# One scan sequence over eight images, and a bound on where TensorE's other products may stand between its state sums

## The chip, the cores and the metric

The kernel runs on one core of one Trainium2 chip. The time is the device time of one execution in microseconds, and the profile is that of one further execution on the same core. All arithmetic is float32.

## What is computed

The reference is a chain of four layers on a batch of eight images of 384 channels and 32x32 pixels. Layer 0 is a state-space block (Mamba) run in both directions over the 1024 pixels, with a gated local branch. Layer 1 is a pointwise and depthwise convolution, linear attention and an MLP. Layers 2 and 3 are large depthwise convolutions (folded into one 13x13 kernel each), a pointwise product and a GELU. Cut to what the kernel's stages show:

```python
# layer 0, per image and direction; d = 384 channels, n = 16 states
xz = einsum('blc,ec->ble', x, in_proj_w);  u, z = split(xz, 2)
u = silu(causal_conv4(u) + b)
dt, Bm, Cm = split(einsum('blc,ec->ble', u, x_proj_w), [24, 40])
delta = softplus(dt @ dt_proj_w.T + dt_proj_b)
h = exp(delta * A) * h + delta * u * Bm      # a scan over 1024 pixels
y = (einsum('bdn,bn->bd', h, Cm) + u * D) * silu(z)
x = x + res_scale * (xn * sigmoid(dwconv3(xn) + dw_b) + scale_mod * (y @ out_proj_w.T))
# layer 1
x = x + c2(dwconv3(c1(x)));  x = x + proj(linear_attention(qkv(x)))
x = x + gelu(layernorm(x) @ w1 + b1) @ w2 + b2
# layers 2 and 3
x = sum of seven depthwise convolutions with batch norm
x = pointwise(x) + x;  out = gelu(dwconv13(x) + scaled x)
```

## The kernel before

All work of layers 0 and 1 is written out by one Python function, `_layers01`, and a compile-time scheduler decides the order of the instructions of each engine: it follows priorities in program order and its own estimate of when inputs are ready, and it puts in the semaphores. [...] The lists are fixed when the program is built.

**The scan of one image.** `scan(b)` walks over 12 units: direction d, half h of the pixels (512 columns), chunk c of 128 channels. A unit has four rounds, so an image has 48 rounds and the batch 384. A round handles four of the sixteen states. Its work is, for each of two halves i:

- ScalarE computes `da`, the exponentials of delta times A, in two instructions of 128x512 (L776), from `dlt`. The tag `da` has 4 buffers, two rounds' worth.
- VectorE multiplies `vr` by the broadcast `bct` into `du`, which lies in PSUM (L781), and runs two scans of 128x512 into `hs` (L793). In the first half of the pixels it copies the end state to `carry` (L798).
- GpSimd multiplies `hs` by the other part of `bct` (L802). The tag `hs` has 8 buffers, four rounds' worth.
- TensorE adds the four states of each channel with four packed products of 128x32 (L736) into `acc`; this is `sums`, and it runs two rounds late, from the list `late`. At the first round of a unit `acc` also takes `y0` (L741). After the unit's fourth round `acc` is copied out (direction 0, `yt`, L746) or multiplied by the gate and stored as `g` (direction 1, L749 and L750).

The scan's inputs are loaded by SP's DMA queue: `load` brings `dlt` and `vr` of the next unit (tag `rep`), `load_bc` the rows `bct`. At the end of an image the two remaining `sums` are written out, and the next image's `scan` starts with its own loads.

**The other work.** While image b is scanned, two generators are advanced: `front(b + 1)`, which is layer 0 ahead of the scan (norm `ms`, products `in`, the local branch `lc` and `lg` at L611 to L620, the causal convolution `c`, `xd`, `dt`, the softplus at L671 to L678, and the stores of delta at L685), and `layer1(b - 1)`, which is the end of layer 0 (`op`, from `g`) and all of layer 1 (`h`, `dw`, `c2`, the attention's `kv_kp`, `kv_vt`, `kvs`, `q`, `den`, `rzb`, `pj`, then `mu`, `var`, and the MLP's `mf` and `mo`). Each yields a cost after a piece of work. `fold` and `kernels` prepare weights during the first images. The driver advances them by a common ratio after each round:

```python
while work and done < need * (i + 1) / (rounds - 1):
    w = min(work, key=lambda w: w[2] / w[1])
    cost = next(w[0], None)
```

`tick` runs small pieces that were put off by `defer`. What a round writes out of this work is thus set by the driver, but where the scheduler then puts it on TensorE's list is not bound to the round.

**After the scans.** `layer1` of image 7 runs alone, and then layers 2 and 3 as convolutions from Toeplitz blocks (`cv_a`, `pw`, `cv_b`, L316 and L347).

[...]

Of the kernel before, what the change touches and what calls it, by code (L numbers as in the profile page):

```python
# [1 line left out]

# [6 lines left out]
FP = mybir.dt.float32  # L9
AF = mybir.ActivationFunctionType  # L10
ALU = mybir.AluOpType
# [3 lines left out]
P = 128  # L15
C = 384
NC = C // P
# [3 lines left out]
HALF = 512  # L21
# [353 lines left out]
def _layers01(tc, nc, B, xv, x2_d, dram, ident, mean_w, eps5, eps6, one, half, minus1, vec, bns, bnt,  # L375
# [12 lines left out]
    with ExitStack() as ctx:  # L388
        wp = ctx.enter_context(tc.tile_pool(name="w0", bufs=1))
        sp = ctx.enter_context(tc.tile_pool(name="s0", bufs=2))  # L390
# [28 lines left out]
        def const(ap, shape, tag):  # L419
            t = wp.tile(shape, FP, tag=tag, name=tag)  # L420
            nc.scalar.dma_start(t, ap)
            return t
# [9 lines left out]
            nc.gpsimd.memset(spread[32 * j : 32 * j + 1, j, :], 1.0)  # L432
        t1 = const(taps1, [P, 2 * NG, 32], "t1")
        selt = const(sel, [P, 32], "selt")
        neg_a = const(alog, [P, NG, NR], "neg_a")
        nc.scalar.activation(neg_a, neg_a, AF.Exp)
        nc.vector.tensor_scalar_mul(neg_a, neg_a, -1.0)
# [55 lines left out]
        def tick(everything=False):  # L493
            for e in list(late):
                e[0] -= 1
                if e[0] < 0 or everything:
                    late.remove(e)
                    e[1]()

        def dense(ps, w, m, rhs):  # L500
            for k in range(NC):
# [14 lines left out]
        def rows(t):  # L516
            return t.rearrange("p (h w) -> p h w", w=W)
# [54 lines left out]
        def front(b):  # L572

            xn = []
# [34 lines left out]
            for h in range(2):  # L609
                for c in range(NC):  # L610
                    xr = t2(f"xr_{b}_{h}_{c}")  # L611
                    nc.sync.dma_start(xr, xv[b][:, c, bass.ts(h, HALF)])
                    ps = conv3(xn_d, b % 2, h, c, t3, f"lc_{b}_{h}_{c}")
                    lc = t2(f"lg_{b}_{c}_{h}")
                    nc.scalar.activation(lc, ps, AF.Sigmoid, bias=vec("dw_b0", c))

                    def local(h=h, c=c, lc=lc, xr=xr):
                        nc.vector.tensor_mul(rows(lc), rows(lc), xn[h][c])
                        nc.vector.scalar_tensor_tensor(xr, lc, rs, xr, ALU.mult, ALU.add)
                        nc.gpsimd.dma_start(x1v[b][:, c, bass.ts(h, HALF)], xr)  # L620

                    defer(1, local)
                    yield 3
# [68 lines left out]
                    defer(1, deltas)  # L692
                    yield 3

        def scan(b):

            units = [
                (d, h, c)
                for d in range(2) for h in ((0, 1) if d == 0 else (1, 0)) for c in range(NC)
            ]  # L700
            late = []
# [2 lines left out]
                return t.rearrange("p (j n) -> p j n", n=HALF)  # L704

            def load_bc(k, r):
                d, h, _ = units[k]
                t = sp.tile([P, 2, HALF], FP, tag="bct", name=f"bct_{b}_{d}_{h}_{r}", bufs=4)
                for o in range(2):
                    src = bass.AP(  # L710
                        bc_d.tensor, bc_d[b, d, o * NST + 4 * r, h * HALF].offset,
                        [[0, 32], [L, 4], [1, HALF]],
                    )
                    nc.sync.dma_start(t[:, o, :], src)
                return t

            def load(k, i):

                d, h, c = units[k]
# [12 lines left out]
            def sums(k, r, hs, acc, y0, zt):  # L732
                d, h, c = units[k]
                cols = bass.ts(h, HALF)
                for j in range(4):
                    nc.tensor.matmul(  # L736
                        acc[32 * j : 32 * j + 32, :], selt, hs[j // 2][:, bass.ts(j % 2, HALF)],
                        start=(r == 0), stop=(r == NR - 1), skip_group_check=True,
                    )
                if r == 0:  # L740
                    nc.tensor.matmul(acc, ident, y0, start=False, stop=False, skip_group_check=True)  # L741
# [13 lines left out]
            for k, (d, h, c) in enumerate(units):  # L755
                cols = bass.ts(h, HALF)
                second = k % (2 * NC) >= NC
                for r in range(NR):
# [11 lines left out]
                    end = HALF - 1 if d == 0 else 0  # L770
                    for i in range(2):
                        dlt, vt = now[i]
                        da = sp.tile([P, 2 * HALF], FP, tag="da", name=f"da_{b}_{k}_{r}_{i}", bufs=N_DA)
                        for j in range(2):
                            g = 4 * c + 2 * i + j
                            nc.scalar.activation(  # L776
                                da[:, bass.ts(j, HALF)], dlt[:, bass.ts(j, HALF)], AF.Exp,
                                scale=neg_a[:, g, r : r + 1],
                            )
                        du = accp.tile([P, 2 * HALF], FP, tag="du", name=f"du_{b}_{k}_{r}_{i}")  # L780
                        nc.vector.tensor_mul(  # L781
                            pairs(du), pairs(vt),
                            bct[r][:, 0:1, :].to_broadcast([P, 2, HALF]),
# [5 lines left out]
                        t = sp.tile([P, 2 * HALF], FP, tag="hs", name=f"hs_{b}_{k}_{r}_{i}", bufs=N_HS)  # L789
# [86 lines left out]

        def layer1(b):

            xx = []
            w = wtile(outproj_t, f"wo_{b}")  # L880
            for h in range(2):
                xh, gh = a6(f"xx_{b}_{h}"), a6(f"g_{b}_{h}")
                nc.sync.dma_start(xh, x1v[b][:, :, bass.ts(h, HALF)])
                nc.sync.dma_start(gh, gv[b][:, :, bass.ts(h, HALF)])
                xx.append(xh)
                for m in range(NC):
                    ps = long_psum(f"op_{b}_{m}_{h}")
                    dense(ps, w, m, gh)
                    o = xh[:, m, :]
                    nc.vector.scalar_tensor_tensor(o, ps, rsm, o, ALU.mult, ALU.add)  # L890
                    yield 3
            w = wtile(c1_d, f"c1_{b}")
            for h in range(2):
# [195 lines left out]
            tick()  # L1089
        tick(everything=True)  # L1090
        rounds = 4 * NC * NR
        for b in range(B):
            work = []
            if b + 1 < B:
                work.append([front(b + 1), 90, 0])
            if b > 0:
                work.append([layer1(b - 1), 325, 0])
            if b == 0:
                work.append([fold(), 30, 0])
            if b == 1:  # L1100
                work.append([some(prepare, 7), 1, 0])
            elif b > 1:
                work.append([some(prepare, 6), 12, 0])
            need = sum(n for _, n, _ in work)
            done = 0
            for i, _ in enumerate(scan(b)):
                tick()

                while work and done < need * (i + 1) / (rounds - 1):
                    w = min(work, key=lambda w: w[2] / w[1])  # L1110
                    cost = next(w[0], None)
                    if cost is None:
                        work.remove(w)
                        continue
                    w[2] += cost
                    done += cost
            for w in work:
                for _ in w[0]:
                    tick()
            tick(everything=True)  # L1120
        for _ in prepare:
            pass
        for _ in layer1(B - 1):
# [90 lines left out]
```

## Time and profile before

| | us |
|---|---|
| three runs | 5799.74, 5803.92, 5806.63 |
| median | 5803.92 |
| the profiled execution | 5806.88 |
| its span, first to last instruction | 5805.1 |
| first scan of image 0 | 215.6 |
| first scan of image 1 | 735.4 |
| first scan of image 7 | 4164.3 |
| last scan of image 7 | 4648.0 |
| granted clock of TensorE, mean | 0.896 of full |
| table loads of ScalarE | 776 of 1.283 |

Engines are PE (TensorE products), PEld (its weight loads), DVE (VectorE), ACT (ScalarE), POOL (GpSimd) and SP (the queue of most loads). A number such as L736 is a line of the kernel before. In the list of 40 slices each digit is the busy share of a fortieth of the span (145 us) in tenths. A wait is written as who waited, an arrow, and the work that ended the wait. A `sums` product is recorded as two instructions, as is every product here. The start of a round is the start of its first scan (L793) in the timeline of VectorE.

### The profile page before, as it was taken

Reading aid. Unit: us, or ns where it says so; the run is one execution under the profiler, and the core shown is the slowest. Engines: PE = TensorE matmul, PEld = TensorE weight load, DVE = VectorE, ACT = ScalarE, POOL = GpSimd, SP = SyncE. Lnnn points to the kernel's source line nnn. Section 1 sums busy time; section 2 is a strip of 40 time slices with the busy share of each in tenths; the row PEclk is TensorE's granted clock in tenths of the full one; section 3 lists DMA queues with packets and bytes.
Section 4 is the critical chain, followed back from the end, with each engine's and each line's share of the span. In section 5 each row is a group of like instructions: output and inputs, shape, how many; then the busy total and the mean of one; then the engine's idle time right before and its main releaser. Section 6 shows DMA issues by size and latency. Waiting matters only on the chain. (4 is left out here: it accounts for less than half of the span.)

```text
span 5805.1 us, 57844 instructions
## 1 busy us (share of the span) xinstructions
PE 4813.5 (83%) x19550; PEld 2091.8 (36%) x19550; DVE 3677.1 (63%) x3775; ACT 3064.5 (53%) x4116; POOL 2892.9 (50%) x1603
## 2 busy tenths in 40 slices
PE   4576579977988799879888997899779869899999
PEld 1121124322332243223322332233223324498498
DVE  0399997968687768776878786878678811011211
ACT  1656546874667557846784687468635613000211
POOL 3277676557554656565656564656466700110133
PEclk7687689988999899989999998899889989999999
DMA  9555476677567756764666467646643541366677
GB/s 299 185 176 178 145 247 194 230 188 216 187 197 202 216 173 193 168 204 134 191 205 189 141 175 186 190 140 176 179 145 120 135 96 45 95 165 158 196 166 150
DMA packets 528255, 1012.16 MB, mean 174 GB/s; under 512 B 60616, under 2 KB 196248, under 8 KB 527960
## 3 DMA queue, kind: packets, MB, share of 16 engines
q1 hardware_dynamic: 387952, 665.99, 38.5%
q0 software_dynamic: 71136, 248.53, 16.6%
q10 hardware_dynamic: 68872, 93.95, 5.1%
q8 instruction: 155, 2.54, 0.2%
q14 instruction: 140, 1.15, 0.1%
HBM read 763.86 MB, written 288.36 MB: 181 GB/s over the span
## 5 line engine op out<-in xcount | busy, mean ns | idle before, releaser
L802 POOL TENSOR_TENSOR hs<-hs,bct 128x1024 f32<-128x1024 f32 x768 | 2378.7, 3098 | 1180.4 <-DVE hs L793 665.8
L776 ACT ACTIVATE da<-dlt,neg_a 128x512 f32<-128x512 f32 x1536 | 1031.7, 714 | 848.8 <-DVE hs L793 756.8
L793 DVE TENSOR_TENSOR_SCAN hs<-da,carry,du 128x512 f32<-128x512 f32 x768 | 947.1, 1268 | 445.8 <-PE acc L736 211.0
L781 DVE TENSOR_TENSOR du<-vr,bct 128x1024 f32<-128x1024 f32 x768 | 1048.3, 1365 | 51.7 <-issue 21.7
L793 DVE TENSOR_TENSOR_SCAN hs<-da,du 128x512 f32<-128x512 f32 x768 | 901.2, 1208 | 153.9 <-ACT da L776 74.0
L736 PE MATMUL acc<-hs,selt 128*32 128x512 f32 x3072 | 736.5, 674 | 293.0 <-POOL hs L802 241.7
L1064 PE MATMUL mo<-hm,w 128*128 128x512 f32 x1152 | 562.5, 628 | 84.4 <-ACT hm L1062 60.8
L502 PE MATMUL mf<-ln,w 128*128 128x512 f32 x1152 | 545.7, 614 | 42.8 <-ACT dl L672 40.4
L736 PEld LDWEIGHTS acc<-hs,selt 128*32 128x32 f32 x3072 | 122.3, 115 | 722.2 <-POOL hs L802 391.6
L1064 PEld LDWEIGHTS mo<-hm,w 128*128 128x128 f32 x1152 | 214.9, 197 | 427.8 <-issue 255.1
L776 ACT ACT_TABLE_LOAD x265 | 340.0, 1283 | 39.2 <-DVE hs L793 26.7
L502 PEld LDWEIGHTS mf<-ln,w 128*128 128x128 f32 x1152 | 215.2, 194 | 358.9 <-issue 285.1
L316 PE MATMUL cv_b<-xt_b,toep 128*64 128x256 f32 x2688 | 304.5, 388 | 14.1 <-DVE xt_b L298 14.1
L316 PE MATMUL cv_a<-xt_a,toep 128*64 128x256 f32 x2688 | 304.6, 388 | 9.2 <-DVE xt_a L298 9.2
L502 PE MATMUL in<-xn,win 128*128 128x512 f32 x576 | 289.1, 633 | 26.0 <-ACT phi_k L874 24.2
L511 PE MATMUL dw<-dw_i,t3b 96*32 96x512 f32 x1152 | 238.0, 707 | 86.4 <-DMA dw_i<-h_d 86.3
L316 PEld LDWEIGHTS cv_b<-xt_b,toep 128*64 128x64 f32 x2688 | 282.5, 199 | 36.6 <-issue 16.2
L316 PEld LDWEIGHTS cv_a<-xt_a,toep 128*64 128x64 f32 x2688 | 282.4, 199 | 31.1 <-issue 10.4
L511 PE MATMUL lc<-lc_i,t 96*32 96x512 f32 x1152 | 218.1, 679 | 57.2 <-issue 28.8
L511 PE MATMUL c<-ut,t 128*32 128x512 f32 x768 | 195.2, 676 | 45.6 <-DMA ut<-u_d 32.1
L502 PE MATMUL op<-g,wo 128*128 128x512 f32 x288 | 143.1, 647 | 86.7 <-DMA g<-g_d 58.7
L1062 ACT ACTIVATE hm<-mf,biasf 128x512 f32<-128x512 f32 x192 | 130.7, 687 | 145.2 <-PE mf L502 143.5
(189 smaller groups left out, 5618.3 us busy)
## 6 DMA issues: line engine op xcount, KB each, us to landing
dlt<-dl_d SPq DMA_DIRECT2D x384, 256.0 KB, 4.5
vr<-v_d SPq DMA_DIRECT2D x384, 256.0 KB, 4.7
bct<-bc_d SPq DMA_DIRECT2D x256, 256.0 KB, 4.1
ut<-u_d SPq DMA_DIRECT2D x192, 257.5 KB, 5.0
lc_i<-xn_d SPq DMA_DIRECT2D x192, 228.8 KB, 4.9
dw_i<-h_d SPq DMA_DIRECT2D x192, 228.8 KB, 4.1
tp_d<-g_d POOLq DMA_DIRECT2D x64, 672.0 KB, 7.2
w<-w_d SPq DMA_DIRECT2D x64, 576.0 KB, 5.8
```

The lines of the kernel that those rows point to most:

```text
L316: nc.tensor.matmul(ps[2 * H * e : 2 * H * (e + 1), 0:BW], tp[:, 2 * (g % (GB // 2)) + e, :, :, t].rearrange("p c j -> p (c j)"), rhs, star ...
L502: nc.tensor.matmul(ps, w[:, k, m * P : (m + 1) * P], rhs[k] if isinstance(rhs, list) else rhs[:, k, :], start=(k == 0), stop=(k == NC - 1),)
L511: nc.tensor.matmul(ps[32 * j : 32 * j + 32, :], lhs(j, i), rhs(j, i), start=(i == 0), stop=(i == taps - 1), skip_group_check=True,)
L736: nc.tensor.matmul(acc[32 * j : 32 * j + 32, :], selt, hs[j // 2][:, bass.ts(j % 2, HALF)], start=(r == 0), stop=(r == NR - 1), skip_group ...
L776: nc.scalar.activation(da[:, bass.ts(j, HALF)], dlt[:, bass.ts(j, HALF)], AF.Exp, scale=neg_a[:, g, r : r + 1],)
L781: nc.vector.tensor_mul(pairs(du), pairs(vt), bct[r][:, 0:1, :].to_broadcast([P, 2, HALF]),)
L793: nc.vector.tensor_tensor_scan(t[:, s][:, way], da[:, s][:, way], du[:, s][:, way], k_c if second else 0.0, ALU.mult, ALU.add,)
L802: nc.gpsimd.tensor_mul(pairs(t), pairs(t), bct[r][:, 1:2, :].to_broadcast([P, 2, HALF]))
L1062: nc.scalar.activation(hm, ps, AF.Gelu, bias=biasf[:, NC * i + f, :])
L1064: nc.tensor.matmul(acc[m], wb[:, f, m * P : (m + 1) * P], hm, start=(i == 0 and f == 0), stop=(i == FF // C - 1 and f == NC - 1),)
```

## The change

There are five edits.

1. `scan` becomes one generator over all 8x12 units. The loads of the next image's first unit are written out in the last rounds of the image before, as between any two units, and the `sums` of the last two rounds of an image are written out in the first rounds of the next.
2. In TensorE's order, products of the other work that are written out after round i are placed behind the `sums` that stand second to last in the list `summed` at that time (`LAG` = 1), which are those of round i-3. The four products of each `sums` are placed behind the last TensorE instruction of the other work written out two rounds before (`BEHIND` = 2), that is, in the same round as the scan that they add up. Both are edges for the scheduler on one engine's list; no semaphore is added for them.
3. Each generator of the driver has its own pace between a first and a last round: `front` from 0 to 43, `layer1` from 3 to 47. At round 43 everything deferred is written out.
4. `layer1` takes half 1 before half 0 in its first two products, `op` and `h`.
5. The sigmoid of the local branch is written as a tanh: sigmoid(v) = (1 + tanh(v/2))/2. The product with `xn` takes the added one, and the residual takes half the scale. Four multiplies of one column at the start make the halved constants.

The core of the diff:

```diff
+LAG = 1
+BEHIND = 2
...
+        def order(ins, before):
+            tc.add_manual_dep(
+                ins, before.name,
+                mybir.DependencyInfo(mybir.DependencyClass.NoSync, mybir.DependencyReason.DATA),
+            )
...
-                    nc.scalar.activation(lc, ps, AF.Sigmoid, bias=vec("dw_b0", c))
+                    nc.scalar.activation(lc, ps, AF.Tanh, bias=dwh[:, c, :], scale=0.5)
...
-                        nc.vector.tensor_mul(rows(lc), rows(lc), xn[h][c])
-                        nc.vector.scalar_tensor_tensor(xr, lc, rs, xr, ALU.mult, ALU.add)
+                        nc.vector.scalar_tensor_tensor(
+                            rows(lc), rows(lc), one, xn[h][c], ALU.add, ALU.mult
+                        )
+                        nc.vector.scalar_tensor_tensor(xr, lc, rsh, xr, ALU.mult, ALU.add)
...
-        def scan(b):
+        def scan():
             units = [
-                (d, h, c)
+                (b, d, h, c) for b in range(B)
                 for d in range(2) for h in ((0, 1) if d == 0 else (1, 0)) for c in range(NC)
             ]
...
+                after = between[-BEHIND] if len(between) >= BEHIND else []
                 for j in range(4):
-                    nc.tensor.matmul(
+                    ins = nc.tensor.matmul(
                         acc[32 * j : 32 * j + 32, :], selt, hs[j // 2][:, bass.ts(j % 2, HALF)],
                         start=(r == 0), stop=(r == NR - 1), skip_group_check=True,
                     )
+                    for o in after:
+                        order(ins.ins, o)
...
+                summed.append(ins.ins)
...
-            for h in range(2):
+            for h in (1, 0):
                 xh, gh = a6(f"xx_{b}_{h}"), a6(f"g_{b}_{h}")
...
+        last = rounds - NR + 1
+        summed = []
+        between = []
+        scans = scan()
         for b in range(B):
             work = []
             if b + 1 < B:
-                work.append([front(b + 1), 90, 0])
+                work.append([front(b + 1), 90, 0, last - 2, 0])
             if b > 0:
-                work.append([layer1(b - 1), 325, 0])
+                work.append([layer1(b - 1), 325, 3, rounds - 1, 0])
...
+            for i in range(rounds):
+                next(scans)
                 tick()
+                ends = []
+                with tc.issue_after(summed[-1 - LAG]) if len(summed) > LAG else nullcontext():
+                    for w in list(work):
+                        gen, need, lo, hi, done = w
+                        at = len(traced())
+                        while done < need * (i + 1 - lo) / (hi - lo) or i >= hi:
+                            cost = next(gen, None)
...
+                        mine = [t for t in traced()[at:] if t.engine == mybir.EngineType.PE]
+                        if mine:
+                            ends.append(mine[-1])
+                between.append(ends)
+                if i == last - 2:
+                    tick(everything=True)
```

More of the change, by code (lines that the diff above doesn't have):

```diff
@@ L1 @@
-from contextlib import ExitStack
+from contextlib import ExitStack, nullcontext
 import concourse.bass as bass
@@ L434, in _layers01 @@
         selt = const(sel, [P, 32], "selt")
+        dwh = wp.tile([P, NC, 1], FP, tag="dwh", name="dwh")
+        for c in range(NC):
+            nc.vector.tensor_scalar_mul(dwh[:, c, :], vec("dw_b0", c), 0.5)
+        rsh = wp.tile([P, 1], FP, tag="rsh", name="rsh")
+        nc.vector.tensor_scalar_mul(rsh, rs, 0.5)
         neg_a = const(alog, [P, NG, NR], "neg_a")
@@ L498, in tick, with traced @@
                     e[1]()
+        def traced():
+            return nc.cur_bb.bb.instructions
+        def order(ins, before):
[3 more added lines that the diff above has]
+            )
         def dense(ps, w, m, rhs):
@@ L706, in load_bc @@
             def load_bc(k, r):
-                d, h, _ = units[k]
+                b, d, h, _ = units[k]
                 t = sp.tile([P, 2, HALF], FP, tag="bct", name=f"bct_{b}_{d}_{h}_{r}", bufs=4)
@@ L717, in load @@
             def load(k, i):
-                d, h, c = units[k]
+                b, d, h, c = units[k]
                 ts = []
@@ L732, in sums @@
             def sums(k, r, hs, acc, y0, zt):
-                d, h, c = units[k]
+                b, d, h, c = units[k]
                 cols = bass.ts(h, HALF)
+                after = between[-BEHIND] if len(between) >= BEHIND else []
                 for j in range(4):
-                    nc.tensor.matmul(
+                    ins = nc.tensor.matmul(
                         acc[32 * j : 32 * j + 32, :], selt, hs[j // 2][:, bass.ts(j % 2, HALF)],
@@ L739, in sums @@
                     )
+                    for o in after:
+                        order(ins.ins, o)
                 if r == 0:
-                    nc.tensor.matmul(acc, ident, y0, start=False, stop=False, skip_group_check=True)
+                    ins = nc.tensor.matmul(acc, ident, y0, start=False, stop=False, skip_group_check=True)
+                summed.append(ins.ins)
                 if r < NR - 1:
@@ L754, in scan @@
             acc = y0 = zt = nxt = None
-            for k, (d, h, c) in enumerate(units):
+            for k, (b, d, h, c) in enumerate(units):
                 cols = bass.ts(h, HALF)
@@ L772, in scan @@
                         dlt, vt = now[i]
-                        da = sp.tile([P, 2 * HALF], FP, tag="da", name=f"da_{b}_{k}_{r}_{i}", bufs=N_DA)
+                        da = sp.tile([P, 2 * HALF], FP, tag="da", name=f"da_{k}_{r}_{i}", bufs=N_DA)
                         for j in range(2):
@@ L779, in scan @@
                             )
-                        du = accp.tile([P, 2 * HALF], FP, tag="du", name=f"du_{b}_{k}_{r}_{i}")
+                        du = accp.tile([P, 2 * HALF], FP, tag="du", name=f"du_{k}_{r}_{i}")
                         nc.vector.tensor_mul(
@@ L788, in scan @@
                             bct[NR - 1] = load_bc(k, NR - 1)
[L789 removed]
+                        t = sp.tile([P, 2 * HALF], FP, tag="hs", name=f"hs_{k}_{r}_{i}", bufs=N_HS)
                         for j in range(2):
@@ L877, in layer1 @@
         def layer1(b):
-            xx = []
+            xx = [None, None]
             w = wtile(outproj_t, f"wo_{b}")
-            for h in range(2):
+            for h in (1, 0):
                 xh, gh = a6(f"xx_{b}_{h}"), a6(f"g_{b}_{h}")
@@ L884, in layer1 @@
                 nc.sync.dma_start(gh, gv[b][:, :, bass.ts(h, HALF)])
-                xx.append(xh)
+                xx[h] = xh
                 for m in range(NC):
@@ L892, in layer1 @@
             w = wtile(c1_d, f"c1_{b}")
-            for h in range(2):
+            for h in (1, 0):
                 hh, mid = image6(f"hh_{b}_{h}")
@@ L1094, in _layers01 @@
             if b + 1 < B:
-                work.append([front(b + 1), 90, 0])
+                work.append([front(b + 1), 90, 0, last - 2, 0])
             if b > 0:
-                work.append([layer1(b - 1), 325, 0])
+                work.append([layer1(b - 1), 325, 3, rounds - 1, 0])
             if b == 0:
-                work.append([fold(), 30, 0])
+                work.append([fold(), 30, 0, rounds - 1, 0])
             if b == 1:
-                work.append([some(prepare, 7), 1, 0])
+                work.append([some(prepare, 7), 1, 0, last, 0])
             elif b > 1:
[L1103 to L1106, printed above, removed]
+                work.append([some(prepare, 6), 12, 0, rounds - 1, 0])
+            for i in range(rounds):
+                next(scans)
                 tick()
[L1109 to L1120, printed above, removed]
+                ends = []
[5 more added lines that the diff above has]
+                            cost = next(gen, None)
+                            if cost is None:
+                                work.remove(w)
+                                break
+                            done += cost
+                            w[4] = done
+                        mine = [t for t in traced()[at:] if t.engine == mybir.EngineType.PE]
[4 more added lines that the diff above has]
+                    tick(everything=True)
+        next(scans, None)
+        tick(everything=True)
         for _ in prepare:
```

## The prediction

> **What bounds the kernel now.** I read, in this order: the busy shares and the 40 slices, the windows by image and by stretch, the waits of VectorE, the timeline of VectorE where it stands longest, and the order of the built programs.
>
> ```profile
> span 5805.1 us, 57844 instructions
> PE 4813.5 (83%) x19550; PEld 2091.8 (36%) x19550; DVE 3677.1 (63%) x3775; ACT 3064.5 (53%) x4116; POOL 2892.9 (50%) x1603
> ...
> PE   4576579977988799879888997899779869899999
> ...
> DVE  0399997968687768776878786878678811011211
> ACT  1656546874667557846784687468635613000211
> ```
>
> From slice 3 to slice 32 no engine is full: TensorE, VectorE and ScalarE share the load and wait for each other. This is the scan stage, 8 images of 48 rounds, 215.6 to 4648.0 us in the timeline. A round of the scan (two `du`, four scans) costs VectorE 2x1.365 + 4x1.24 = 7.7 us by the rows of L781 and L793, and the shortest rounds last 7.6 us; 48 of them would be 365 us, while images 1 to 6 take 3428.9/6 = 571.5 us each. The next view is VectorE's waits in these six images (735.4 to 4164.3 us): us in all, times, longest.
>
> ```profile
> DVE hs L793 <- ACT da L776: 236.6, 79, 16.4
> DVE hs L793 <- PE acc L736: 218.6, 48, 19.1
> DVE dl L683 <- ACT sp L678: 59.8, 22, 11.0
> DVE xx L890 <- PE op L502: 41.5, 7, 17.7
> ```
>
> Half of what the scan waits for is TensorE's state sums (they free the `hs` buffers), half is ScalarE's exponentials. The windows of image 5, cut after rounds 11, 20 and 35 (columns: length, then busy of PE, PEld, DVE, ACT, POOL, then clock, DMA):
>
> ```profile
> 3023.90:3132.50 108.60, 85.21 (x332) 29.86 (x333) 102.61 (x119) 61.22 (x92) 81.35 (x41) 0.86 0.66 210
> 3132.50:3260.00 127.50, 112.03 (x399) 48.45 (x393) 78.04 (x62) 60.68 (x93) 60.11 (x27) 0.93 0.41 124
> 3260.00:3417.00 157.00, 146.20 (x562) 51.72 (x564) 139.81 (x153) 116.92 (x144) 95.49 (x38) 0.92 0.63 194
> 3417.00:3589.40 172.40, 150.55 (x435) 49.32 (x432) 117.95 (x103) 140.69 (x169) 95.25 (x52) 0.94 0.68 175
> ```
>
> The first stretch is VectorE's, the second TensorE's, the last ScalarE's. The second holds one round of 42 us, which VectorE's timeline shows:
>
> ```profile
> 3203.99 2.45 DVE L793 TENSOR_TENSOR_SCAN hs<-da,carry,du 128x512 f32<-128x512 f32 x2 [18.90 <-PE acc L736]
> 3206.47 1.23 DVE L781 TENSOR_TENSOR du<-vr,bct 128x1024 f32<-128x1024 f32 x1
> 3220.88 2.45 DVE L793 TENSOR_TENSOR_SCAN hs<-da,carry,du 128x512 f32<-128x512 f32 x2 [13.17 <-PE acc L736]
> ```
>
> In the order of the program before, 116 products of other images stand between the sums of rounds 12 and 13; the scan, four rounds of `hs` buffers ahead, runs into them at round 16. That is the loss the change can reach.
>
> [...] the trace has 1283 ns on every load and the next activation about 0.02 us behind it, so I price 1.283. [...]
>
> **The change part by part.** Loads of each engine are counted from the built order (what stands between one round's scan work and the next on that engine) times durations of this trace: a 128x512 product 2x0.429 us at full clock and divided by 0.93, four packed sums 0.9, a table load 1.283, other work by its row.
>
> *Table sets.* Sigmoid becomes tanh: 776 loads become 676 in the built programs, 128 us of ScalarE, some 13 us per image of 397. The activation stays (0.687 us at L615). The product at L618 (mean 1490 ns) becomes a fused one like L619 (824 ns): 48 of them, between 0 and 32 us of VectorE, inside the loads below; I take 0. Four multiplies of one column (like L158, 0.16 us) lie under the first image's front.
>
> *One sequence.* Loads for the next image's first unit, eight of 256 KB, and its `bct` move from after an image's end to its rounds 45 to 47 on SP's queue; they land in 4.1 to 4.7 us, and the `rep` and `bct` buffers come free at the scan's pace as inside an image. [...] The stores of the front that they read (POOL's queue, behind a 3.1 us multiply each) are flushed at round 43. I cost the move at 0. Rounds 0 and 1 lasted 16 and 12 to 29 us, partly by the 41.5 us on `op`; `layer1` now begins at round 3, with the half whose `g` was stored three units earlier, so that wait goes (it is inside the stretches below).
>
> *The binding.* Products lie at most about three rounds ahead of the sums; the largest block between sums is 49 small ones. By stretches of a steady image, load before (and what it lasted) and after, in us, the largest engine:
> - before: rounds 0-11 DVE 116 (108.6); 12-20 PE 129 (127.5); 21-35 DVE 152 (157); 36-47 ACT 147 (172.4).
> - after: rounds 0-8 DVE 86 (PE 83); 9-20 PE 109 (DVE 100); 21-30 DVE 112 (PE 94); 31-43 ACT 188 (DVE 126, PE 119); 44-47 DVE 41.
>
> The first three stretches before lasted 0.99 of their largest load (393 of 397), so rounds 0 to 30 after give 0.99x307 = 304. Two things are added. First, what the binding costs: sums of round r now stand behind the products traced with round r. In eleven rounds (nine of 9-20, and 27, 28) the built semaphores make sums r wait, through ScalarE's order, for a scan of round r+3, while scan r+4 needs sums r: no slack. The long chain is two exponentials 1.4, a square 0.6, two kv products 3.9, kvs and sums 1.5, six hand-overs of an estimated 0.2 (a weight load is 0.19): 8.6, and 2.5 of scan, 11.1 us a round, some 3.2 over what VectorE needs; the short chain is 7.1 and free. All short costs 0, nine long 29; half, **14 us**. Second, ScalarE's stretch: 188 us at 1.17 (as 172.4/147) is 220, at full density 188; TensorE is lighter there than before (119 in 13 rounds, where it was busy 151 of 172), so I take the middle, **203**. Sum: 304 + 14 + 203 + 41 = **562 us**, against 571.5: -9.5, six times, **-57**.
>
> *Image 7* has `layer1` alone: its rounds 0-1 lasted 43 us and 12-15 72 us, with loads of 20 and 44 in the new order; less 16 us of the chain, **-35** (-15 to -45). Image 0 (450 and 452 us of VectorE), `layer1` of the last image and the convolutions stay: 0.
>
> Sum -92. The profiled run took 5806.88 us (span 5805.1), the median of three is 5803.92, 3 less: 5803.9 - 92 = **5712 us**. Ends per image: 304+0+188+41 = 533 (-231 and -45: 5528) and 304+29+220+41 = 594 (+135 and -15: 5924).
>
> **The rivals.**
> 1. *The order was the only loss*: chain hidden, ScalarE dense; 533 per image, 5528 to about 5560. For it: TensorE is level in the new order. Against: ScalarE's own density in the last stretch is 141 of 172.
> 2. *Slower: the binding turns TensorE's waits into the scan's.* In rounds 8 to 20 sums stand behind products that wait for ScalarE or for `dw` images (TensorE waited 122 us in all for these, 15 per image, formerly with other products to run). Chain 29 and dw 15 on top of 304+203+41: 592, +20.5 six times, less 20 for image 7: +103, about **5905**. It decides from some 29 us per image. For it: eleven rounds without slack. Against: rounds without slack also stand in the MLP of image 7 before and last 7.6 to 10 us.
> 3. *ScalarE takes over*: 1.17 holds, 579 per image, +45-35: 5814, no change.
> 4. *The binding does nothing*: excluded by the built order (116 to 49).
>
> **How the numbers follow.** Forecast 0.38, rival 1 0.20, rival 3 0.10, rival 2 0.32. Below 0.2% (12 us) no measurement of this kernel tells a change. Faster 0.58, within 0.09, slower 0.33. The likeliest case alone spans 5640 to 5780; the 8-in-10 range, 5570 to 5880, cuts the outer parts of rivals 1 and 2.
>
> **What would show it.** Right: VectorE's wait for `acc` in images 1 to 6 falls from 218.6 to about 100 and no round is over 25 us; table loads 676; rounds 31-43 last 190 to 220 us with ScalarE the busiest; the wait for `da` does not fall. Wrong: rounds 9-20 above 140 us (rival 2), or rounds 31-43 below 185.

## The result, and the profile after

The changed kernel is slower. It takes 6067.73 us (median of four runs, 6058.21 to 6077.94), the kernel before on the same chip 5805.16: a ratio of 1.0454, 95% interval 1.0434 to 1.0475. The forecast was 5712 with a range up to 5880, so the result lies past the range and past the slower rival (5905). The profiled execution took 6062.94 us.

The head of the page after, and three of its rows of 40 slices:

```profile
span 6061.2 us, 57648 instructions
PE 4853.6 (80%) x19550; PEld 2093.5 (35%) x19550; DVE 3649.8 (60%) x3779; ACT 2921.7 (48%) x4016; POOL 2939.3 (48%) x1603
...
PE   5565568876878788878897887788769879899899
...
DVE  0488976858675867686778686768678821011211
ACT  1644525674457645754595568456834623100211
```

The engines do nearly the same work as before: TensorE is busy 40 us more (its granted clock was 0.880 on average, before 0.896), GpSimd 46 us more, VectorE 27 us less, ScalarE 143 us less (the hundred table loads that are gone, at 1.283 us each 128 us). So most of the 256 us of span are waiting, not work. By parts, from first scan to first scan:

| part | before | after |
|---|---|---|
| before the first scan | 215.6 | 219.8 |
| image 0 | 519.8 | 533.6 |
| images 1 to 6 | 3428.9 | 3657.7 (609.6 each, before 571.5) |
| image 7 | 483.7 | 489.0 |
| after its last scan | 1157.1 | 1161.1 |

Nine tenths of the loss are in the six steady images. The next table gives the mean length of stretches of an image there, in us, cut where the two kernels differ.

| rounds | 0-9 | 10-13 | 14-22 | 23-30 | 31-43 | 44-47 | sum |
|---|---|---|---|---|---|---|---|
| before | 109 | 36 | 112 | 98 | 159 | 58 | 572 |
| after | 94 | 71 | 93 | 122 | 196 | 33 | 609 |

Three stretches became shorter, 59 us together: the start of an image, the stretch with the 42 us round, and the end. Three became longer, 97 us together. What is awaited there stands in TensorE's waits of the changed kernel in images 1 to 6 (753.4 to 4411.1 us; us in all, times, longest):

```profile
PE dw L528 <- DMA dw_i<-h_d: 138.4, 27, 24.9
PE c L528 <- DMA ut<-u_d: 115.6, 15, 21.6
PE mo L1090 <- ACT hm L1088: 93.8, 51, 11.1
PE var_b L581 <- ACT var_r L578: 66.7, 12, 7.7
PE lc L528 <- DMA t<-in_taps: 51.2, 6, 10.4
```

Before, the same two rows for `dw` and `ut` read as follows, and `lc` had none for its weights `t`:

```profile
PE dw L511 <- DMA dw_i<-h_d: 63.3, 29, 5.5
PE c L511 <- DMA ut<-u_d: 23.3, 13, 3.5
```

The three waits for a DMA grew by about 218 us together, and the six images by 229. That the two are close proves nothing, since the rows of `mo` and `var_b` grew as well (from 40.7 and 25.8); what the waits cost is for the experiments to say. The six images in VectorE's waits of the changed kernel:

```profile
DVE hs L819 <- PE acc L759: 349.8, 69, 17.5
DVE hs L819 <- ACT da L802: 263.1, 80, 26.6
DVE lg L635 <- ACT lg L632: 115.1, 12, 20.0
DVE xx L946 <- ACT c L943: 100.4, 18, 10.5
```

The wait for the sums has risen from 218.6 to 349.8 instead of falling to 100. The last two rows are new near the top: VectorE itself stands behind the gate of the local branch (`lg`, fed by `lc`) and the residual after `c2` (fed by `dw`), with scans queued behind them. Rounds of over 25 us, of which the forecast expected none, are 13 in these six images, where there were 9; most are round 12, 23, 38 or 39.

**Rounds 11 and 12**, 21.2 and 23.5 us in image 5. The timeline of all engines there, of which I show the DMA issues, and then TensorE's own (start, length, operation, and in brackets the idle time ahead and what ended it):

```profile
3296.94 0.38 ACTq L547 DMA_DIRECT2D h_d<-hh  x1
...
3301.63 3.78 SPq L558 DMA_DIRECT2D dw_i<-h_d  x6
```

```profile
3307.02 6.22 PE L528 MATMUL dw<-dw_i,t3b 96*32 96x512 f32 x27 [15.16 <-DMA dw_i<-h_d]
...
3320.48 1.92 PE L528 MATMUL dw<-dw_i,t3b 96*32 96x512 f32 x2 [4.41 <-DMA dw_i<-h_d]
```

`h` goes to DRAM at 3296.9, comes back as shifted images from 3301.6, and the first product starts at 3307.0: 10 us of round trip. TensorE has stood for 15 us by then, since this product is next on its list. Only six images are on their way at once (the tag `im` has 6 buffers, and a product takes four), so the next products wait too (4.41 us). VectorE in the same rounds:

```profile
3320.63 1.23 DVE L807 TENSOR_TENSOR du<-vr,bct 128x1024 f32<-128x1024 f32 x1
3335.57 2.45 DVE L819 TENSOR_TENSOR_SCAN hs<-da,carry,du 128x512 f32<-128x512 f32 x2 [13.71 <-PE acc L759]
```

The scan waits 13.71 us for sums that stand behind `dw`.

**Round 23**, 28.0 us in image 5 and 28 to 36 in the six, is the wait for the tap weights `t` of `lc`. TensorE stands for them, and VectorE then waits for the gate that the `lc` products feed; the next scan, at 3488.3 us, is behind this gate in its order. First TensorE, then VectorE's row of `lg` between 3455 and 3492 us:

```profile
3471.28 5.68 PE L528 MATMUL lc<-lc_i,t 96*32 96x512 f32 x28 [8.87 <-DMA t<-in_taps]
```

```profile
DVE lg L635 <- ACT lg L632: 15.8, 2, 9.1
```

**Round 38**, 34.5 us. The x2 stores leave on POOL's queue and the loads of `ut` on SP's, at the same time:

```profile
3669.66 2.33 POOL L1102 DMA_DIRECT2D x_d<-xx  x2
...
3673.06 3.56 SPq L656 DMA_DIRECT2D ut<-u_d  x4
...
3698.02 3.81 PE L528 MATMUL c<-ut,t 128*32 128x512 f32 x4 [20.42 <-DMA ut<-u_d]
...
3704.67 1.28 DVE L819 TENSOR_TENSOR_SCAN hs<-da,carry,du 128x512 f32<-128x512 f32 x1 [25.91 <-ACT da L802]
```

A `ut` load has a median of 4.9 us over the whole program. These four took 24.9 to 26.2 us to land, TensorE stands for 20.42, and the scan 25.91. The scan does not wait for these products; ScalarE's timeline shows how it comes to them:

```profile
3701.86 0.69 ACT L664 ACTIVATE uc<-c,pk 128x512 f32<-128x512 f32 x1 [22.99 <-PE c L528]
3702.57 1.28 ACT L802 ACT_TABLE_LOAD   x1
3703.86 0.72 ACT L802 ACTIVATE da<-dlt,neg_a 128x512 f32<-128x512 f32 x1
```

The exponentials stand behind the activation of `c` in ScalarE's order, and that waits 22.99 us; their own row shows no wait. One late load thus stops three engines in turn, for 20.42, 22.99 and 25.91 us.

The windows of image 5, cut after rounds 11, 20 and 35 (columns as in the prediction), answer to those shown of before:

```profile
3218.20:3335.60 117.40, 87.24 (x342) 31.23 (x342) 97.30 (x113) 49.79 (x77) 81.32 (x35) 0.88 0.63 199
3335.60:3444.00 108.40, 101.03 (x372) 41.06 (x370) 73.36 (x60) 60.93 (x89) 59.72 (x26) 1.00 0.41 129
3444.00:3636.00 192.00, 164.45 (x634) 57.39 (x632) 148.16 (x160) 115.47 (x151) 100.39 (x42) 0.91 0.56 179
3636.00:3806.10 170.10, 131.96 (x380) 45.54 (x378) 114.41 (x105) 135.38 (x167) 94.39 (x55) 0.89 0.61 168
```

Only the second, the attention's rounds, was improved by more than a few us (127.5 to 108.4), and TensorE is again busy for most of it. In the third no engine is full.

### The profile page after: what moved, and what is told of

Read it like the earlier page. It is cut to its first block, busy times and chain, and to the rows that moved or that the text cites. A ratio compares the mean times of both kernels' runs of the same rounds, so it can differ in the third digit from the quotient of the medians.

```text
span 6061.2 us, 57648 instructions
## 1 busy us (share of the span) xinstructions
PE 4853.6 (80%) x19550; PEld 2093.5 (35%) x19550; DVE 3649.8 (60%) x3779; ACT 2921.7 (48%) x4016; POOL 2939.3 (48%) x1603
## 5 line engine op out<-in xcount | busy, mean ns | idle before, releaser
L828 POOL TENSOR_TENSOR hs<-hs,bct 128x1024 f32<-128x1024 f32 x768 | 2427.5, 3161 | 1563.3 <-DVE hs L819 760.7
L807 DVE TENSOR_TENSOR du<-vr,bct 128x1024 f32<-128x1024 f32 x768 | 1005.3, 1309 | 26.7 <-DMA vr<-v_d 14.5
L759 PE MATMUL acc<-hs,selt 128*32 128x512 f32 x3072 | 642.6, 646 | 215.5 <-POOL hs L828 196.4
L1090 PE MATMUL mo<-hm,w 128*128 128x512 f32 x1152 | 579.1, 643 | 118.5 <-ACT hm L1088 118.5
L519 PE MATMUL mf<-ln,w 128*128 128x512 f32 x1152 | 558.9, 623 | 23.5 <-ACT dl L691 23.5
L528 PE MATMUL lc<-lc_i,t 96*32 96x512 f32 x1152 | 233.6, 746 | 128.3 <-DMA t<-in_taps 51.2
L759 PEld LDWEIGHTS acc<-hs,selt 128*32 128x32 f32 x3072 | 96.0, 111 | 609.8 <-POOL hs L828 337.6
L635 DVE SCALAR_TENSOR_TENSOR lg<-lg,one,xn 128x512 f32<-128x512 f32 x48 | 72.9, 1519 | 258.4 <-ACT lg L632 243.0
```

The lines of the kernel that those rows point to most:

```text
L519: nc.tensor.matmul(ps, w[:, k, m * P : (m + 1) * P], rhs[k] if isinstance(rhs, list) else rhs[:, k, :], start=(k == 0), stop=(k == NC - 1),)
L528: nc.tensor.matmul(ps[32 * j : 32 * j + 32, :], lhs(j, i), rhs(j, i), start=(i == 0), stop=(i == taps - 1), skip_group_check=True,)
L635: nc.vector.scalar_tensor_tensor(rows(lc), rows(lc), one, xn[h][c], ALU.add, ALU.mult)
L759: ins = nc.tensor.matmul(acc[32 * j : 32 * j + 32, :], selt, hs[j // 2][:, bass.ts(j % 2, HALF)], start=(r == 0), stop=(r == NR - 1), skip ...
L807: nc.vector.tensor_mul(pairs(du), pairs(vt), bct[r][:, 0:1, :].to_broadcast([P, 2, HALF]),)
L828: nc.gpsimd.tensor_mul(pairs(t), pairs(t), bct[r][:, 1:2, :].to_broadcast([P, 2, HALF]))
```

## The experiments

All ratios are to the kernel before, run on the same chip at the same time, with 95% intervals. The kernel before took 5763 to 5810 us on the chips used, so where two changed kernels are set against each other, it is their ratios that are compared.

### Which edit costs: the two edges and the tanh

`e1_unbound` keeps all of the change but the edges (edit 2):

```diff
-                after = between[-BEHIND] if len(between) >= BEHIND else []
+                after = []
...
-                with tc.issue_after(summed[-1 - LAG]) if len(summed) > LAG else nullcontext():
+                with nullcontext():
```

> The changed kernel with both edges on TensorE's order taken out: one sequence, own paces, half 1 first and tanh stay. Theory A (the binding makes TensorE's waits for DMA-fed images the scan's waits): most of the 262 us go, 5780 to 5860 us, and TensorE's wait for dw images and ut images (254 us over images 1 to 6 in the changed kernel) falls to under 130. Theory B (writing the next image's loads and the paces into one sequence costs by itself): 6000 to 6070. Theory C (ScalarE's order in rounds 31 to 43 decides): within 1% of the changed kernel, since ScalarE's work is the same.

Measured 1.0305 [1.0281, 1.0328], 5940.45 us, which fits none of the three theories: the loss is neither all in the edges nor untouched by them. TensorE's waits in images 1 to 6 show what the edges do:

```profile
PE c L528 <- DMA ut<-u_d: 118.5, 23, 21.6
PE dw L528 <- DMA dw_i<-h_d: 44.3, 18, 6.8
PE lc L528 <- DMA t<-in_taps: 23.2, 4, 7.5
```

With the edges `dw` waits 138.4 and `lc` 51.2 us. The wait for `ut` is as long without them (115.6 with), so it has another cause.

`e2_lag_only` has only the first of these two edits and so keeps only the bound on how far ahead the other products may stand; `e3_behind_only` has only the second and keeps the bound on how far behind; `e4_behind4` sets `BEHIND = 4`.

> The changed kernel with only the edge that puts the sums behind the other products (BEHIND) taken out; other products still may not run ahead of the sums by more than three rounds. Theory A: the sums need not wait for a product that waits for DMA, but a late product can still stand ahead of them by the scheduler's choice: 5800 to 5900. Theory B: 6000 to 6070. Theory C: within 1% of the changed kernel.

> The changed kernel with only the other edge (LAG) taken out; sums still stand behind the products written out in the round of their scan. Theory A: as slow as the changed kernel or slower, 6030 to 6150, since this edge is the one that ties the sums to a late product. Theory B: 6000 to 6070. Theory C: within 1%.

> The changed kernel with BEHIND = 4: sums of round r stand behind the products of round r-2 instead of r. Theory A: a product has two more rounds (16 us) for its images to land before it holds the sums; 5830 to 5930, VectorE's wait for acc in images 1 to 6 from 350 to under 200 us. Theory B: 6000 to 6070. Theory C: within 1%.

Measured 1.0364 [1.0341, 1.0386], 1.0476 [1.0454, 1.0498] and 1.0349 [1.0329, 1.0369]. Theory A had promised larger gains for the first and the third, though in `e4_behind4` VectorE's wait for the sums fell to 156.6 us, as it said; that the second is no faster than the changed kernel was to be expected by A and C alike. So a third of the loss, 1.5 points, is the binding, and three points are there without it. Within the binding the edge that holds sums behind the other work is the costly one: alone it costs as much as both, and two rounds more of slack give 1.0 point back. By stretches the edges mostly move time: from e1 to the change rounds 0-9 go from 103 to 94 us, 14-22 from 107 to 93, 31-43 from 207 to 196 and 44-47 from 54 to 33, while 10-13 go from 38 to 71 and 23-30 from 88 to 122. An image is 13.5 us longer on balance.

`e5_tanh` is the kernel before with edit 5 alone.

> The kernel before with only the tanh in place of the sigmoid (and its two fused products). If the tanh and the order that the scheduler then finds were the cost of the unbound sequence: 5860 to 5940. If the cost lies in the sequence or the paces: 5730 to 5790 (some 100 table loads less, 128 us of ScalarE, of which little lies on the path).

Measured 1.0099 [1.0076, 1.0122]: an edit that takes 89 table loads from ScalarE (776 to 687 in the trace) makes the kernel slower by 1%.

### The pace and the one sequence

`e6_pace` is e1 with one scan generator per image, as before (edit 1 undone). `e7_bind_only` has the edges, the tanh and half 1 first (edits 2, 4 and 5), with the scan per image and the common pace of the kernel before.

```diff
-        def scan():
+        def scan(b):
...
-        scans = scan()
         for b in range(B):
+            scans = scan(b)
```

> The unbound changed kernel (e1) with one scan per image again, so that an image's first loads and its last two sums stand where they stood before; the own paces (front by round 43, layer1 from 3 to 47), half 1 first and tanh stay. If the paces cost (softplus and MLP packed into rounds 31 to 43 on ScalarE): as slow as e1, ratio 1.02 to 1.04. If the joined sequence costs: ratio 0.99 to 1.01.

> The kernel before with tanh, half 1 first and both edges on TensorE's order, but with one scan per image and the common pace of before. Theory A, binding makes TensorE's waits the scan's, costing what it cost the sequence (1.5%): ratio 1.01 to 1.02. If binding cures the 42 us round and the sequence is what costs: ratio 0.97 to 0.99.

Measured 1.0393 [1.0366, 1.0421] and 1.0204 [1.0184, 1.0224]. The one sequence by itself is a gain of 0.9 point (e6 to e1). From e5 to e6, which adds the own paces (with the flush at round 43) and half 1 first, the loss grows by 2.9 points, the largest step of all; half 1 first was not run alone. The growth stands in rounds 31 to 43, which go from 165 to 204 us, while rounds 0 to 30 last 344 us in both. TensorE's wait for `ut` in images 1 to 6 goes from 39.4 to 142.0 us. So this wait comes with the paces, not with the edges. Against e5 the edges with half 1 first cost 1.05 points on the old pace.

### Room for the depthwise products

TensorE waits for the round trip of `h` because the pace writes `dw` out right behind it and the edges keep it there: in image 5 the `dw` products stand in rounds 10 to 12, in e1, with the same pace, in rounds 10 to 15. `e8_gap` writes out some two rounds of nothing after `h` is stored and spreads `dw` wider, with the pace's total raised by the same 46:

```diff
+            yield 16
...
-                    yield 3
+                    yield 8
...
-                work.append([layer1(b - 1), 325, 3, rounds - 1, 0])
+                work.append([layer1(b - 1), 371, 3, rounds - 1, 0])
```

> The changed kernel with 16 units of nothing between the store of h and the first dw product, and each dw product counted as 8 units in place of 3, so that the images' loads (6 buffers) have the time of a round each. Theory A: TensorE's wait for dw images in images 1 to 6 falls from 138 to under 60 us and rounds 10 to 13 from 71 to under 50 us; total 5960 to 6020. If the waits on dw only stand where another wait would stand: within 0.5% of the changed kernel.

Measured 0.9964 [0.9951, 0.9977], 5785.21 us: 4.9 points come back, far more than the 5960 to 6020 us expected. TensorE's waits in images 1 to 6 of e8 (the row of `ut` is no longer among the first ten):

```profile
PE mo L1091 <- ACT hm L1089: 148.8, 52, 20.1
PE kvs L984 <- ACT vt L978: 46.1, 11, 8.0
PE var_b L581 <- ACT var_r L578: 41.5, 12, 4.2
PE dw L528 <- DMA dw_i<-h_d: 33.3, 19, 3.8
```

But the edit does two things, since all that follows `dw` also comes later against `front`. `e9_shift` puts the 46 behind `c2` instead, so that `dw` stays crowded and the later work lies about where e8 has it.

> The changed kernel with 46 units of nothing put after c2 instead of around dw (e8 put 16 ahead of dw and 30 between its products). dw is as crowded as in the changed kernel; everything after c2 stands where it stands in e8. If dw's loads were the loss: 5980 to 6080, dw wait 100 to 140 us. If the shift of the later work against the front (its lc and c products, the stores of x2) was the gain of e8: 5780 to 5860.

Measured 1.0115 [1.0097, 1.0133], between the two expectations. So the later place of the work after `dw` is worth 3.4 points, and the room for `dw` 1.5. The split is a rough one, since the larger total also makes `layer1` run faster through its first part: `dw` stands in rounds 10 and 11 alone there. In e9 rounds 23-30 fall from 122 to 95 us and 31-43 from 196 to 179, and `dw` waits 68.7 us; in e8 rounds 10-13 fall to 36, what they were before the change. In both kernels the last six `ut` loads of image 5 stand at rounds 39 and 40 and the first x2 store at 41; in the changed kernel loads and stores meet at 38, and in e1 and e6 at 39.

### The x2 store

The x2 store writes rows of 32 pixels, 128 bytes, into a padded image. `e10_rows` stores the same bytes of the changed kernel as 2-KB rows into another scratch, and `e13_before_rows` does this in the kernel before; layers 2 and 3 then read zeros, with the same instructions, and no longer wait for the store.

```diff
-                            x2v[
-                                m, :, h * (H // 2) : (h + 1) * (H // 2),
-                                PADW + b * (W + PADW) : PADW + b * (W + PADW) + W,
-                            ],
-                            rows(o),
+                            x2s[b][:, m, bass.ts(h, HALF)], o,
```

> The changed kernel with layer1's result stored in rows of 2 KB in a scratch tensor instead of rows of 128 bytes in x2; layers 2 and 3 then read zeros, with the same instructions. Those 48 stores take 16.9 us to land. If they hold up the ut loads of the front and so TensorE (116 us of waits in images 1 to 6): the ut wait falls under 50 us, rounds 37 to 39 from 69 to under 50, total 5900 to 5990. If ut waits for buffers or SP's queue: within 0.5% of the changed kernel.

Measured 1.0087 [1.0072, 1.0102], 5859.76 us, a larger gain than expected. The issues of this store (KB each, median us from issue to landing), in the changed kernel and then in e10:

```profile
x_d<-xx POOLq DMA_DIRECT2D x48, 256.0 KB, 16.9
```

```profile
x2s_d<-xx POOLq DMA_DIRECT2D x48, 256.0 KB, 5.2
```

And TensorE's row of `ut` in e10, against 115.6 above:

```profile
PE c L529 <- DMA ut<-u_d: 20.3, 12, 6.1
```

The landings say the same: of the 109 `ut` loads of images 1 to 6 whose landing is on record, 15 took over 12 us in the changed kernel (26.5 at most) and none in e10 (10.9 at most); in e1 they were 14, and before none. So the short rows, where they meet these loads, explain the `ut` wait. Whether they explain the loss needs the kernel before with the same edit.

> The kernel before with layer1's result stored in rows of 2 KB in a scratch tensor, as in e10 (layers 2 and 3 read zeros). In the changed kernel this took 3.5%. If most of that is the meeting of the stores with the front's ut loads in round 38, the kernel before, where they stand apart, gains under 1.5%: ratio 0.985 to 1.0. If the stores cost any order as much: ratio 0.96 to 0.97.

Measured 0.9771 [0.9754, 0.9787], between the two expectations. The kernel before also gains 2.3 points, of the 3.7 that the changed one gains. So most of this cost was there all along, and some 1.4 points of the loss go with the meeting of store and loads that the change brought about. A steady image gains 27 us in e10 and 14 in e13. After the last scan the span is 29 and 18 us shorter; that part lies ahead of the convolutions, which take 304 or 305 us each in all four traces, so the zeros that they read don't show.

### Which parts are worth keeping

`e11_gap_unbound` is e8 without the edges, `e12_gap_sigmoid` e8 with the sigmoid, `e14_gap_unbound_sigmoid` both, and `e15_before_gap` the kernel before with the same 46 units of room.

> e8 with both edges on TensorE's order taken out. If binding only costs where a bound product waits for its data, it now costs little and the level order is a gain: e11 slower than e8, 5800 to 5900. If binding costs by itself: e11 faster than e8, 5690 to 5770.

> e8 with the sigmoid and its products of before in place of the tanh. If tanh costs 1% here as it did alone (e5): 5715 to 5740, faster than both kernels. If the cost in e5 was an accident of the order: within 0.5% of e8, or slower by the 100 table loads (up to 30 us).

> The one sequence with own paces and half 1 first, dw given room (e8), no edges (e11) and the sigmoid of before (e12). If the two gains over e8 add (1.1% and 0.65%): ratio 0.978 to 0.982, 5680 to 5710. If they are one gain seen twice: 0.985, as e11.

> The kernel before with only the room around dw (16 units ahead, 8 for each product). If that room alone is the gain, with one scan per image and the common pace: ratio 0.97 to 0.985. If it needs the one sequence (the first rounds of an image and the early loads): ratio 0.99 to 1.01.

| kernel | edges | function | ratio | interval |
|---|---|---|---|---|
| e8 | yes | tanh | 0.9964 | 0.9951 to 0.9977 |
| e11 | no | tanh | 0.9853 | 0.9837 to 0.9870 |
| e12 | yes | sigmoid | 0.9899 | 0.9880 to 0.9918 |
| e14 | no | sigmoid | 0.9888 | 0.9871 to 0.9904 |
| e15 (before) | no | sigmoid | 1.0003 | 0.9994 to 1.0013 |

e11, at 5726.61 us, beats both kernels, as the theory that binding costs by itself had it; e12 and e14 lie between or beside their expectations, and e15 is as expected if the room needs the one sequence. With the tanh the edges cost 1.1 points here too; with the sigmoid they cost nothing that shows. The tanh costs 0.65 point with the edges and is no loss without them. So neither has a fixed price. That each acts through the order that the scheduler then finds is likely but not shown: the orders were not compared. The room for `dw` is worth nothing in the kernel before (e15) and pays with the new sequence and paces. VectorE's waits in images 1 to 6 of e8, and then of e11:

```profile
DVE hs L819 <- PE acc L759: 402.6, 72, 26.6
DVE hs L819 <- ACT da L802: 66.0, 29, 5.2
```

```profile
DVE hs L819 <- ACT da L802: 145.9, 52, 10.5
DVE du L807 <- DMA vr<-v_d: 126.3, 18, 15.6
DVE hs L819 <- PE acc L759: 116.3, 38, 7.0
```

The bound program waits for the sums, 402.6 us; the unbound one much less (116.3), and it meets the loads of `vr` instead. But e8 waits for the sums longer than the changed kernel (349.8) and is 4.9 points faster. So this wait, which the forecast took as its first sign, does not measure the loss.

## Why the prediction was wrong, point by point

**The loss that was to be cured is cured.** The round of 42 us is gone (rounds 14-22: 112 to 93 us), VectorE's wait for `op` is shorter (41.5 to 32.6) and rounds 0-9 fell from 109 to 94. Table loads are 676. For rounds 14-22 e1 against the change shows that the edges do this: without them they last 107. But they are not the only cure: e11, with room for `dw` and no edges, has 92 there. The chain without slack was put at 11.1 us a round, and rounds 13 to 20 last 9 to 14, 10.8 on average; in e1 they last 11.8, so this match does not show the chain. In other places new long rounds arose.

**The step that failed is "rounds 0 to 30 give 0.99x307 = 304".** With the chain it made 318 us; measured are 380. Rounds 31-43 were put at 203 and last 196, rounds 44-47 at 41 and last 33. The 62 us too few in the first term, less the 15 too many in the other two, are the 47 us by which an image missed (609.6 for 562). In the forecast's own stretches: rounds 0-8 last 87 us (forecast 85), 9-20 154 (108), 21-30 140 (111). The sign that was named for rival 2, rounds 9-20 above 140, has come.

**Why it failed: the edges.** In e1 rounds 0 to 30 last 335 us. So 45 of the 62 us come with the edges, and 17 are missing without them. The forecast's likeliest sum gave the loads of `dw` and `lc` no cost at all. Bound to their rounds, these products stop the sums of the same rounds while they wait for a load: from e1 to the change TensorE's wait for `dw` grows by 94 us and that of `lc` for its weights by 28, and rounds 10-13 and 23-30, where they stand, last 34 us more each. The wait for `ut` is no part of this: it lies in rounds 31 to 43, and e1 has it too.

**Why it failed: the factor.** The 0.99, length over the largest engine's load, was read from the kernel before, and from counted loads. The count is too high: it gives VectorE 116 us in rounds 0 to 11, which lasted 108.6 in image 5, and the forecast's own windows show VectorE busy for 102.61. By these windows the busiest engine worked 102.61, 112.03 and 146.20 us in the three stretches (TensorE in the third, not VectorE), 361 of 393, a factor of 1.09. With it 307 would have become 335, which is what e1 takes; as the 307 was counted in the same way, that may be chance.

**Rival 2 had the right mechanism for the edges, and less than half the size.** It priced `dw` at 15 us per image; rounds 10-13 grew by 35. It did not name the tap weights of `lc` (rounds 23-30, +24 on the kernel before). Its mechanism is also not all of the loss: e1 loses 3.05% with no binding, and the largest step is that of the paces.

**Rounds 31-43: a good number for a bad reason.** They were to last 190 to 220 us because ScalarE fills them. They last 196, but in the window of rounds 36 to 47 ScalarE is busy 135.38 of 170.1 us, and e10 takes the stretch to 177 with ScalarE's work unchanged. The paces moved the last `c` products of `front` to rounds 38 and 39, where the x2 store lies; without the edges the stretch lasts 207. The forecast moved them on paper without asking what else is on the DMA engines then. In the wait of 20.42 us in image 5 (3677.6 to 3698.0 us) these are busy for 0.96 of the time and move 100 GB/s; over the six images they are busy for 0.59 and move 177. The store took 16.9 us to land in rows of 128 bytes and 5.2 in rows of 2 KB.

**The tanh was put at zero to a small gain** and costs 1.0% alone (e5). The table loads did go, so what was wrong is that no cost was thought possible; where the 1% comes from stays open.

**The move to one sequence was put at zero** and is a gain of 0.9 point, between e6 and e1. **Image 7** was to gain 35 us and lost 5.

**The sum of the parts, as the runs show it:** tanh +1.0 alone; paces with half 1 first +2.9; one sequence -0.9; edges +1.5: in all 4.5. The steps form one path from the kernel before to the changed one, so their sum closes by construction, and the last table shows that in another order they would have other sizes.

**What stays open.** e9 moves the later work as a whole, so the 3.4 points are not split between the wait of `lc` for its weights and that of `ut`; e10 bounds the second at about 3.7 with the store's own cost in it. Of the 2.9 points of the paces with half 1 first, the meeting of store and loads is a part, 1.4 if it costs as much without the edges as with them; the rest has no cause shown. The 17 us that rounds 0 to 30 lack without the edges were not traced to a wait. The tanh's 1% was not followed into the order. e11 with the store in long rows was not tried, since layers 2 and 3 would have to read another layout.

## What to carry to other kernels

A ratio of length to load read from one order need not hold for another, and a counted load that exceeds the length of its own stretch is a sign to go back to the busy times. Before binding one chain's instructions to another's, list every product whose input comes through DRAM, and ask what the engine has to run in that round trip (it took 10 us for `h` here, and TensorE was idle for 15.16 us ahead of the first `dw` product); if the answer is nothing, leave room first. Here binding gained nothing even then (e8 against e11, e12 against e14). When a change moves loads, look at what else is on the DMA engines at the new place, and at the row size of that (here 16.9 us a store in 128-byte rows and 5.2 in 2-KB rows).

## What the runs showed of the hardware that was not expected

A store of 256 KB in 128-byte rows landed in 16.9 us (16.4 in the kernel before), in 2-KB rows in 5.2 (3.7). It delayed loads of another queue: in round 38 four `ut` loads took 24.9 to 26.2 us to land, where such loads have a median of 4.9, and two `dlt` loads issued behind them took 9.3 and 21.4 us (median 3.8); with long rows no `ut` load of the six images took over 10.9. Forty-eight such stores are worth 2.3% of the kernel before (0.9771 [0.9754, 0.9787]), although TensorE, VectorE and ScalarE have no wait in its images 1 to 6 that ended with one (GpSimd has 39 us, SP's queue 13).
